# Layer 0's tiles with batch 0's tokens first, its queries made beside the others, more side steps per quartet

## The chip, the core and the metric

The kernel runs on one core of one Trainium2 chip. The metric is the device time of one execution in microseconds, given as the median of three runs. The core has a matrix engine (TensorE, PE), three elementwise engines (VectorE or DVE, ScalarE or ACT, GpSimd or POOL) and SyncE (SP), which issues most DMAs. Each engine works through its own queue in order and waits on semaphores for the others.

## The reference

Four batches of 512 tokens of width 256 go through two layers. Each layer is a cross attention to a context and then a mixture of eight experts, each with its own residual:

```python
x = x + L0_xattn(layernorm(x), ctx)   # one head, MLP 256-1024-256
x = x + L0_ffn(layernorm(x))          # top 2 of 8 experts, 256-1024-256, relu, then W_out
x = x + L1_xattn(layernorm(x), ctx)   # 16 heads of 16, softmax over 512 keys
x = x + L1_ffn(layernorm(x))          # top 1 of 8 experts, 256-512-256, gelu, no W_out
```

What matters here is the passage from the second line to the third. For every token `L0_ffn` sums two experts' outputs, weighted by the gates, and multiplies by `W_out`; this is added to x; x is normalized and multiplied by `Wq` to give the queries. Keys and values come from the context and don't depend on x. Everything is float32.

## The kernel before, in words

**Layer 0's experts.** While layer 0's attention and MLP run, every token's row is sent, once per expert chosen, into a region of `sent` in device memory that belongs to that expert. An expert's rows lie there in the order in which they were sent, so batch 0's are the first of each region. A tile is 256 rows of one expert. One tile, of the expert with the most rows so far, is worked while the last batch is still in its MLP (`pick`, `leave`). `plan` then counts for each expert the tiles still needed (`more`, `count`), sums them up (`end`), and writes for tile number i the expert and the first row: all tiles of expert 0, then all of expert 1, and so on. `leave` prepares what `plan` needs of the tile already taken (`used`, `stride`, `full`, `first`). `full[:, 0, 0:1] = -1.0` makes sure that tile 0 is one of expert 0.

`tiles` works 19 tiles (`usual`), and in an `If` four more, should `plan` have counted more. `run` does per tile: hidden layer (`hide`, 16 matmuls of 256 columns, L587; each float32 matmul is two instructions), loads and turn of the next tile, output (`project`, L600), scaling by the gate (L554) and a scatter of the rows from POOL's queue into `came` (L476), where each row's place follows from its token, batch and pick. Then comes one step of the iterator `also`, which clears the first set of attention buffers (`places`) and fetches batch 0's keys and values (`fetch`).

**Layer 1's attention.** `bring` fetches a batch's two sets of output rows from `came`; it can begin when the scatters have landed. `combine` adds the two, turns them (L1043, L1044) and multiplies by `W_out` (L1068, L1069). `prepare` normalizes (L239 to L252), turns, and makes the queries `qc` (L1086, L1089). `place` lays queries and keys of a batch out for the heads by 16 DMAs each (L1103, L999).

There are 16 groups, four of four heads for each batch. For each group the scores are made twice: by query (`sc`), for each query's maximum over the keys (L1133, kept in `nm`), and, two groups later, by key (`scT`) for the exponentials (L1130). `put_greatest` writes the maxima into qT in between, and `weigh` multiplies the exponentials by the values (`av`, L1146). A group is eight quartets of score matmuls, n = 0 to 7; groups -2 and -1 have maxima only. Between quartets stand the side steps, a list of generators worked in order: a `yield k` asks for k quartets to go by before the next step. Before the change there is a place for a step after n = 1, 5 and 7; after every quartet in groups -2 and -1; after even n too in the last batch; and after n = 2 when more than two generators are in the list. `finish` and `choose` (the attention's output and layer 1's gates) of each batch are side work as well.

Ahead of group -2 the kernel does in this order: all `bring`, `combine` of batch 0, `combine` of batch 1, `prepare` and `place` of batch 0, the clearing of the second set of buffers, part of `combine` of batch 2.

**Who sets the order.** Inside the `manual_schedule` block of the attention PE's order is that of the program. Everything else, in the tiles on all engines and in the attention on the others, is put in order by a planner that walks through the program with its own durations and takes, for a free engine, the earliest instruction of the program that it holds to be ready. `keep_in_program_order` binds an instruction to its place. Buffers of pools that follow each other share addresses; a new one waits for all who used the old. Six banks of PSUM hold scores (`ps_pool`), two hold everything else in the attention (`psT`); `av` keeps one of the two for most of a group.

Of the kernel before, what the change touches and what calls it, by code (L numbers as in the profile page):

```python
# [43 lines left out]
def xattn_ffn_kernel(ctx: ExitStack, tc: tile.TileContext, a: dict, out: bass.AP):  # L44
# [116 lines left out]

    falling = const.tile([P, NT, NE], F32, tag="falling", name="falling")
# [3 lines left out]
    def constants():  # L166
# [14 lines left out]

        nc.gpsimd.memset(full[:, 0, 0:1], -1.0)
# [100 lines left out]
    class Dispatch:  # L283


        def __init__(self, layer, pool, n, func, b1_all):
            self.layer, self.pool, self.group = layer, pool, f"send{layer}"
            self.n, self.func, self.b1_all = n, func, b1_all
            self.w1_all, self.w2_all, self.b2_all = (a[f"L{layer}_ffn_{x}"] for x in ("W1", "W2", "b2"))
            self.kept = []  # L290
            self.seen = pool.tile([P, NT + 1, NE], F32, tag="seen0", name="seen0")
            nc.vector.memset(self.seen[:, 0, :], 0.0)
# [82 lines left out]
        def leave(self):  # L375
# [14 lines left out]
            row = pool.tile([P, 1], I32, tag="row_0", name="row_0")  # L390
            nc.vector.tensor_copy(row, start[:, 0:1])
            self.row_0 = row
            self.stride = pool.tile([P, NE], F32, tag="stride", name="stride")
            nc.vector.tensor_tensor(self.stride, start[:, 1 : NE + 1], start[:, 0:NE], ALU.subtract)
            self.full = pool.tile([P, NE, CAP // TT], F32, tag="full_i", name="full_i")
            nc.vector.tensor_tensor(self.full, over(used, CAP // TT), full, ALU.add)
            self.first = pool.tile([P, TILES0], F32, tag="first_i", name="first_i")
            nc.vector.tensor_scalar(self.first, number[:, :, 0], float(TT), start[:, 0:1], ALU.mult, ALU.add)

        def plan(self):  # L400
# [5 lines left out]
            more = small.tile([P, NE, CAP // TT], F32, tag="more", name="more")  # L406
# [5 lines left out]
            past = small.tile([P, TILES0, NE], F32, tag="past", name="past")  # L412
# [12 lines left out]
            nc.vector.tensor_scalar(e, e, float(NE - 1), None, ALU.min)  # L425
# [90 lines left out]
        def tiles(self, n_tiles, usual, tp, midp, pm_pool, po_pool, also):  # L516
# [46 lines left out]
            def run(first, last):  # L563
# [3 lines left out]
                for i in range(first, last):  # L567
# [7 lines left out]
                    next(also, None)  # L575
# [55 lines left out]
    with tc.tile_pool(name="l0a", bufs=2) as lp, tc.tile_pool(name="l0tmp", bufs=2) as tp, tc.tile_pool(  # L631
# [279 lines left out]
        for b in range(B):  # L911
# [9 lines left out]
            if b < B - 1:  # L921
                together(
                    mlps[b], *(part(g, SCORES) for g in near(attends, 2)), *near(gates, -1), *near(filling, 0)
                )
                if b == B - 2:
# [48 lines left out]
    kTs, vas, qTs = [], [], []  # L974

# [33 lines left out]


    with tc.tile_pool(name="f0tmp", bufs=2) as tp, tc.tile_pool(
# [5 lines left out]
        send.tiles(  # L1017
            TILES0, 2 * N // TT + 3, tp, midp, pm_pool, po_pool, early,
        )
# [7 lines left out]
    with tc.tile_pool(name="l1a", bufs=2) as lp, tc.tile_pool(name="l1s", bufs=1) as sp, tc.tile_pool(  # L1027
# [4 lines left out]
        HALF = S // 2  # L1032
        ctxs, qcs = {}, {}
        send = Dispatch(1, fp, H1, AF.Gelu, a["b1_1_col"])

        def flipped(dst, src, name):

            for c in range(NC):
                if c:
                    yield 0  # L1040
                ps = psT.tile([P, S], F32, tag="psT", name=name)
                for t in range(NT):
                    nc.tensor.transpose(ps[:, ts(t, P)], src[:, t, ts(c, P)], ident)  # L1043
                nc.scalar.copy(dst[:, c, :], ps)  # L1044

        back = came[0].rearrange("(k b p t) d -> k b p t d", k=2, b=B, t=NT)
        ys = {}

        def bring(b):

            y = ys[b] = wpool.tile([P, 2, NT, D], F32, tag="w1" if b % 2 else "w2", name=f"y{b}")
            for k in range(2):
                nc.sync.dma_start(y[:, k, :, :], back[k, b])

        def combine(b):

            xb, y = xs[b], ys[b]
            (nc.gpsimd if b else nc.vector).tensor_tensor(y[:, 0, :, :], y[:, 0, :, :], y[:, 1, :, :], ALU.add)  # L1060
            aT = xtp.tile([P, NC, S], F32, tag="xnT", name="aT")
            yield 2
            yield from flipped(aT, y[:, 0, :, :], "psTr4")
            for t in range(NT):
                yield 0
                po = psT.tile([P, D], F32, tag="psT", name="po4")
                for c in range(NC):
                    nc.tensor.matmul(po, aT[:, c, ts(t, P)], w_out[:, c, :], start=c == 0, stop=c == NC - 1)  # L1068
                nc.vector.tensor_tensor(xb[:, t, :], po, xb[:, t, :], ALU.add)  # L1069

        def prepare(b):

            xb = xs[b]
            xn = sp.tile([P, NT, D], F32, tag="xn", name="xn1")
            xnT = xtp.tile([P, NC, S], F32, tag="xnT", name="xnT1")
            qc = qcs[b] = sp.tile([P, NC, S], F32, tag="qc", name="qc", bufs=2)
            normalize(xn, xb, (nc.vector, nc.scalar, nc.gpsimd, nc.gpsimd)[b])
            nc.gpsimd.tensor_tensor(xb, xb, per_token(bo), ALU.add)
            yield 3
            yield from flipped(xnT, xn, "psTr1")  # L1080
            for m in range(NC):
                for at in range(0, S, HALF):
                    yield 0
                    ps = psT.tile([P, HALF], F32, tag="psT", name="pq")
                    for c in range(NC):
                        nc.tensor.matmul(  # L1086
                            ps, wq[:, c, ts(m, P)], xnT[:, c, at : at + HALF], start=c == 0, stop=c == NC - 1
                        )
                    nc.scalar.activation(qc[:, m, at : at + HALF], ps, AF.Identity, bias=bq[:, m : m + 1])  # L1089

        def place(b):

            qT = qTs[b % 2]
            for _ in fetch(b) if b else early:
                pass
# [316 lines left out]
```

## Time and profile before

| what | us |
|---|---|
| median of three runs (1034.33 to 1038.02) | 1034.34 |
| the profiled execution | 1030.9 |
| its span, first to last instruction | 1029.1 |
| tiles of layer 0, from the first `pm` to the last `po` | 311.2 to 584.7 |
| from there to the first `scT` (group 0) | 584.7 to 649.7 |
| groups 0 to 15, to the last copy of `av` | 649.7 to 920.9 |
| busy: PE, DVE, ACT, POOL | 956.2, 531.9, 358.4, 289.4 |

A row of a profile group gives line, engine, operation, what it writes and reads, the shape and the count, then the busy time in us, the mean ns of one, and the idle time of the engine in front of it with what ended it. In a view in order of time each line starts with the start in us, then the duration in us, and in brackets the idle time of the engine just before. In a table by stretches, the columns are busy us of each engine with its count, PE's granted clock (1.00 is full), the DMA engines' share and GB/s. The chain is the work that ended last, followed back from the last instruction.

### The profile page before, as it was taken

Reading aid. Unit: us, or ns where it says so; the run is one execution under the profiler, and the core shown is the slowest. Engines: PE = TensorE matmul, PEld = TensorE weight load, DVE = VectorE, ACT = ScalarE, POOL = GpSimd, SP = SyncE. Lnnn points to the kernel's source line nnn. Section 1 sums busy time; section 2 is a strip of 40 time slices with the busy share of each in tenths; the row PEclk is TensorE's granted clock in tenths of the full one; section 3 lists DMA queues with packets and bytes.
Section 4 is the critical chain, followed back from the end, with each engine's and each line's share of the span. In section 5 each row is a group of like instructions: output and inputs, shape, how many; then the busy total and the mean of one; then the engine's idle time right before and its main releaser. Section 6 shows DMA issues by size and latency. Waiting matters only on the chain.

```text
span 1029.1 us, 14194 instructions
## 1 busy us (share of the span) xinstructions
PE 956.2 (93%) x4883; PEld 642.2 (62%) x4883; DVE 531.9 (52%) x1384; ACT 358.4 (35%) x646; POOL 289.4 (28%) x330
## 2 busy tenths in 40 slices
PE   5879989999998999999999759999999999998996
PEld 3556757675787888888888645433333333447785
DVE  6675585556652222222222167766777777625232
ACT  4435242223122111221112113466655555572331
POOL 3330153234332212211111176021114121033453
PEclk9889999999999999999999979999999999999998
DMA  6779999963344566556665132000111002034682
GB/s 206 224 185 240 251 253 245 251 151 120 117 142 132 190 210 207 177 182 219 210 206 177 54 159 70 13 11 8 45 33 47 25 22 98 26 98 138 208 247 78
DMA packets 113713, 146.05 MB, mean 142 GB/s; under 512 B 15060, under 2 KB 95197, under 8 KB 113632
## 3 DMA queue, kind: packets, MB, share of 16 engines
q1 hardware_dynamic: 106880, 129.24, 44.2%
q0 software_dynamic: 6336, 14.75, 4.4%
q8 instruction: 43, 0.70, 0.3%
q10 hardware_dynamic: 416, 1.05, 0.3%
q14 instruction: 38, 0.31, 0.1%
HBM read 86.71 MB, written 58.80 MB: 141 GB/s over the span
## 4 chain that ended last, share of the span: by engine, by line
PE 67%; DVE 9%; issue 8%; DMA 7%; POOL 7%; SPq 1%; ACT 1%; POOLq 0%; DVEq 0%; ACTq 0%
PE po L600 13%; PE pm L587 12%; PE sc L1126 12%; PE av L1146 5%; PE po L722 5%; PE pm L716 4%; DMA sent<-rows,slot 2%; PE pm_sid L674 2%; DVE nm L1133 2%; PE pf L682 2%; DMA rows<-sent 1%; PE pd L697 1%; PE pt L812 1%; PE pq L1086 1%; PE po L1180 1%
## 5 line engine op out<-in xcount | busy, mean ns | idle before, releaser
L1133 DVE TENSOR_REDUCE nm<-sc 128x1 f32<-128x512 f32 x256 | 164.9, 683 | 59.8 <-PE scT L1126 57.4
L1130 ACT ACTIVATE ex<-scT 128x512 f32<-128x512 f32 x256 | 138.7, 597 | 107.7 <-PE scT L1126 107.3
L587 PE MATMUL pm<-inT,w 128*128 128x256 f32 x736 | 164.0, 380 | 0.8 <-ACT mid L591 0.5
L600 PE MATMUL po<-w,mid 128*128 128x256 f32 x736 | 163.6, 379 | 0.8 <-ACT mid L591 0.8
L1126 PE MATMUL sc<-kT,qT 32*128 32x512 f32 x512 | 152.9, 642 | 3.8 <-DVE nm L1133 3.6
L587 PEld LDWEIGHTS pm<-inT,w 128*128 128x128 f32 x736 | 139.3, 190 | 21.0 <-ACT mid L591 1.6
L1126 PE MATMUL scT<-qT,kT 32*128 32x512 f32 x512 | 149.8, 642 | 0.0
L600 PEld LDWEIGHTS po<-w,mid 128*128 128x128 f32 x736 | 138.0, 190 | 19.0 <-ACT mid L591 1.2
L476 POOL DMA_INDIRECT came<-y,rows x38 | 37.3, 981 | 218.6 <-DVE y L554 218.6
L554 DVE SCALAR_TENSOR_TENSOR y<-po,rows,y 128x256 f32<-128x256 f32 x54 | 26.1, 483 | 133.5 <-PE po L600 125.4
L1126 PEld LDWEIGHTS sc<-kT,qT 32*128 32x128 f32 x512 | 46.5, 183 | 69.5 <-DVE nm L1133 44.3
L242 POOL TENSOR_TENSOR rstd<-var,halved 128x4 f32<-128x4 f32 (+1 forms) x32 | 28.1, 881 | 213.5 <-DVE var L241 207.5
L591 ACT ACTIVATE mid<-pm,b 128x256 f32<-128x256 f32 x108 | 49.9, 471 | 107.4 <-PE pm L587 92.1
L589 DVE TENSOR_SCALAR mid<-pm,b 128x256 f32<-128x256 f32 x76 | 36.8, 484 | 93.0 <-PE pm L587 93.0
L551 ACT ACTIVATE y<-b,rows 128x256 f32<-128x256 f32 x54 | 24.6, 500 | 168.0 <-DMA b<-in_L_ffn_b 121.7
L335 POOL DMA_INDIRECT sent<-rows,slot x48 | 47.5, 990 | 106.0 <-DVE slot L332 32.3
L1146 PE MATMUL av<-ex,va 128*32 128x512 f32 x512 | 69.5, 612 | 0.0
L716 PE MATMUL pm<-hT,w 128*128 128x512 f32 x128 | 62.3, 611 | 0.5 <-DVE hT L629 0.5
L722 PE MATMUL po<-w,mid 128*128 128x256 f32 x256 | 59.2, 381 | 0.0
L722 PEld LDWEIGHTS po<-w,mid 128*128 128x128 f32 x256 | 47.9, 190 | 9.1 <-issue 3.1
L1126 PEld LDWEIGHTS scT<-qT,kT 32*128 32x128 f32 x512 | 45.1, 183 | 4.1 <-issue 3.5
L1146 PEld LDWEIGHTS av<-ex,va 128*32 128x32 f32 x512 | 10.2, 108 | 48.9 <-issue 37.8
(285 smaller groups left out, 1266.1 us busy)
## 6 DMA issues: line engine op xcount, KB each, us to landing
w<-in_L_ffn_W SPq DMA_DIRECT2D x40, 1024.0 KB, 5.4
sent<-nowhere SPq DMA_DIRECT2D x32, 1161.0 KB, 18.8
w<-in_L_ffn_W SPq DMA_DIRECT2D x22, 512.0 KB, 4.3
rows<-sent SPq DMA_DIRECT2D x27, 258.0 KB, 2.9
y<-came SPq DMA_DIRECT2D x8, 512.0 KB, 9.2
b<-in_L_ffn_b SPq DMA_DIRECT2D x28, 128.0 KB, 7.0
x<-in_x SPq DMA_DIRECT2D x4, 512.0 KB
c<-in_ctx SPq DMA_DIRECT2D x4, 512.0 KB
```

The source lines that it names most:

```text
L335: i = nc.gpsimd.indirect_dma_start(out=sent[self.layer][:, :], out_offset=bass.IndirectOffsetOnAxis(ap=slot[:, t - tts[0], k : k + 1], axi ...
L476: i = nc.gpsimd.indirect_dma_start(out=came[self.layer][:, :], out_offset=bass.IndirectOffsetOnAxis(ap=rows[:, u, TO:ROW].bitcast(I32), ax ...
L587: nc.tensor.matmul(pm, w1[:, c, ts(k, P)], inT[:, c, :], start=c == 0, stop=c == NC - 1)
L589: nc.vector.tensor_scalar(mid[:, k, :], pm, bias[:, k : k + 1], 0.0, ALU.add, ALU.max)
L591: nc.scalar.activation(mid[:, k, :], pm, func, bias=bias[:, k : k + 1])
L600: nc.tensor.matmul(po, mid[:, k, ts(t, P)], w2[:, k, :], start=k == 0, stop=k == n - 1)
L716: nc.tensor.matmul(pm, w1_mlp[:, c, ts(k, P)], hT[:, c, :], start=c == 0, stop=c == NC - 1)
L722: nc.tensor.matmul(po, mid[:, k, ts(t, P)], w2_mlp[:, k, :], start=k == 0, stop=k == HD // P - 1)
L1126: nc.tensor.matmul(sc, stay, move, start=True, stop=True)
L1130: nc.scalar.activation(ex, sc, AF.Exp, scale=1.0 / DH**0.5)
L1133: nc.vector.tensor_reduce(nm[:, t, head, 0:1], sc, AX.X, ALU.max, negate=True)
L1146: nc.tensor.matmul(av[32 * head : 32 * head + 32, :], vas[b % 2][:, t, 4 * g + head, :], exs.pop((t, head)), start=t == 0, stop=t == NT - 1,)
```

## The change

1. `leave` splits layer 0's tiles in two parts. `send.zero` keeps how many rows of batch 0 each expert has. `front` is the number of tiles, behind the one already taken, that hold rows of batch 0, and at least one for expert 0 (`least`). The list of tiles now has all front tiles of all experts first, and then the rest in the old order. `plan` adds what lies in front (`in_front`, `e_front`, `first`).
2. The tiles take a function `also(i)` in place of an iterator. Eleven tiles are the most that the front can have (`FRONT`). After tiles 10 and 11, `bring` fetches batch 0's rows, from POOL's queue; from tile 13 on three steps per tile do `combine`, `prepare` of batch 0; after the last tile `place(0)` follows. The fetched rows, the normalized ones and the queries of batch 0 lie in the tiles' own pool. `flipped`, `combine`, `prepare`, `place` and `bring` move ahead of the tiles unchanged but for the pools and the queue.
3. The attention begins with group -2 right after the other `bring`s and the clearing. All of `combine` and `prepare` of batches 1 to 3 is side work, with `place(1)` as a step of the list. There is a place after n = 2 whenever the list isn't empty, and after n = 6 in groups 0 to 4, in the last batch, and when the list has more than two; groups -2 and -1 take two steps per quartet.
4. The buffers of maxima move from the pool `l1s` to `heads`. In `combine` of batch 1 one exponential of one element is taken after the turn.

```diff
-        nc.gpsimd.memset(full[:, 0, 0:1], -1.0)
+        nc.gpsimd.memset(least, 0.0)
+        nc.gpsimd.memset(least[:, 0:1], 1.0)
...
+            front = least
+            past_used = small.tile([P, NE, CAP // TT], F32, tag="past_used", name="past_used", bufs=1)
+            nc.vector.tensor_tensor(past_used, over(used, CAP // TT), full, ALU.add)
+            if self.zero is not None:
+                more = small.tile([P, NE, CAP // TT], F32, tag="more", name="more", bufs=1)
+                front = small.tile([P, NE], F32, tag="front", name="front")
+                nc.vector.tensor_tensor(more, over(self.zero, CAP // TT), past_used, ALU.is_gt)
+                nc.vector.tensor_reduce(front, more, AX.X, ALU.add)
+                nc.vector.tensor_tensor(front, front, least, ALU.max)
...
+            nc.vector.tensor_scalar(end, end, self.in_front, None, ALU.add)
...
-                    next(also, None)
+                    also(i)
...
+                if b == 1:
+                    n, _ = send.counted("n0")
+                    send.zero = fp0.tile([P, NE], F32, tag="zero", name="zero")
+                    nc.vector.tensor_copy(send.zero, n[:, 0, :])
...
+    for i in range(2):
+        nms.append(heads.tile([P, NT, 4, 32], F32, tag=f"nm{i}", name="nm"))
+        nc.gpsimd.memset(nms[i], 0.0)
...
+    FRONT = (2 * S + NE * (TT - 1)) // TT
...
+        def batch0():
+            yield
+            yield from combine(0)
+            yield from prepare(0, tp)
+
+        zero = batch0()
+
+        def also(i):
+
+            next(early, None)
+            if FRONT <= i + 1 < FRONT + 2:
+                bring(0, i + 1 - FRONT, tp, nc.gpsimd)
+            elif i + 1 < usual:
+                together(part(zero, 3 if i > FRONT + 1 else 0))
+            elif i + 1 == usual:
+                together(zero)
+                together(early)
+                place(0)
+
+        send.tiles(TILES0, usual, tp, midp, pm_pool, po_pool, also)
...
-            for b in range(B):
-                bring(b)
-            prepares, combines = ([g(b) for b in range(B)] for g in (prepare, combine))
-            together(combines[0])
-            next(prepares[0])
-            together(combines[1])
-            together(prepares[0])
-            place(0)
+            for b in range(1, B):
+                for k in range(2):
+                    bring(b, k, wpool, nc.sync)
             together(places(sp))
-            next(prepares[1])
-            together(part(combines[2], 3))
-            side += [combines[2], prepares[1], combines[3]]
-            begun.update(side[:2])
+            combines = [None] + [combine(b) for b in range(1, B)]
+            prepares = [None] + [prepare(b, sp) for b in range(1, B)]
...
+            side += [waiting(8), combines[1], prepares[1], placed(1), combines[2], prepares[2], combines[3], prepares[3]]
+            to_place = [2, 3]
...
+                dense = i < NG + 1 or i // NG == B - 1
...
-                    if n == 0 and i >= 0 and i % NG == 0 and i // NG + 1 < B:
-                        place(i // NG + 1)
-                        if i == 0:
-                            side += prepares[2:]
+                    if to_place and i >= (to_place[0] - 1) * NG and prepares[to_place[0]] not in side:
+                        assert i == (to_place[0] - 1) * NG and n <= 3
+                        place(to_place.pop(0))
...
-                    elif n in (1, 5, 7) or i < 0 or (n % 2 == 0 and i // NG == B - 1) or (n == 2 and len(side) > 2):
+                    elif n in (1, 5, 7) or i < 0 or (n % 2 == 0 and i // NG == B - 1) or (n == 2 and side) or (n == 6 and (dense or len(side) > 2)):
                         step()
+                        if i < 0:
+                            step()
```

## The prediction

> **What bounds the kernel now.** I read the page first, then the busy time by stretch around the seam where layer 0's tiles end, then the instructions in order of time in that seam, then the beat of the attention groups. The page: TensorE (PE) is busy nearly everywhere, and the one deep hole after the start is slices 22 and 23.
>
> ```profile
> PE 956.2 (93%) x4883; PEld 642.2 (62%) x4883; DVE 531.9 (52%) x1384; ACT 358.4 (35%) x646; POOL 289.4 (28%) x330
> PE   5879989999998999999999759999999999998996
> PEclk9889999999999999999999979999999999999998
> ```
>
> The stretches (columns: PE, weight loads, DVE, ACT, POOL busy with counts; granted clock; DMA share; GB/s) show what the hole is:
>
> ```profile
> 560.00:584.70 24.70, 24.67 (x117) 21.38 (x115) 5.48 (x11) 3.75 (x8) 2.92 (x3) 1.00 0.36 119
> 584.70:596.30 11.60, 0.00 (x0) 0.00 (x0) 1.77 (x3) 0.00 (x0) 1.11 (x2) 0.70 0.51 177
> 604.00:612.00 8.00, 1.92 (x9) 1.10 (x7) 6.84 (x7) 0.30 (x1) 6.70 (x6) 0.86 0.00 0
> 622.20:636.00 13.80, 13.13 (x61) 6.83 (x60) 12.17 (x27) 4.19 (x8) 5.18 (x4) 1.00 0.25 58
> 688.40:857.40 169.00, 167.87 (x1174) 62.61 (x1174) 125.88 (x255) 100.12 (x189) 33.30 (x32) 1.00 0.10 28
> ```
>
> In the tiles PE has no free time. Then it stands 11.6 us, works a little, stands 6 us, and from 622 to 650 (the two groups whose scores only feed maxima) DVE is nearly full, while PE's "busy" is the modelled length of four-row-group matmuls and not dense. In order of time:
>
> ```profile
> 577.60 7.07 PE L600 MATMUL po<-w,mid 128*128 128x256 f32 x32
> 589.85 3.96 SPq L1055 DMA_DIRECT2D y<-came  x8
> 594.99 1.23 DVE L1060 TENSOR_TENSOR y<-y 128x1024 f32<-128x1024 f32 x1 [4.20 <-DMA y<-came]
> 596.36 1.94 PE L1043 MATMUL psTr<-ident,y 128*128 128x128 f32 x8 [11.69 <-DVE y L1060]
> 606.33 5.24 DVE L252 TENSOR_SCALAR xn<-x,mv,rstd 128x256 f32<-128x256 f32 x4 [1.16 <-POOL rstd L242]
> 622.25 2.80 PE L1126 MATMUL sc<-kT,qT 32*128 32x512 f32 x8
> 649.69 0.69 PE L1126 MATMUL scT<-qT,kT 32*128 32x512 f32 x1
> ```
>
> The last tile ends at 584.67, its rows land at 589.85, come back at 594.9, are combined, normalized, projected to queries and laid out by 622.25; the first group with weights starts at 649.68. **The seam is 65.0 us.** From there PE's own queue is the chain; the copies of av out of PSUM are its beat:
>
> ```profile
> 671.48 0.58 ACT L1295 COPY avs<-av 128x512 f32<-128x512 f32 x1 [0.15 <-PE av L1146]
> 688.42 0.58 ACT L1295 COPY avs<-av 128x512 f32<-128x512 f32 x1
> 754.82 0.58 ACT L1295 COPY avs<-av 128x512 f32<-128x512 f32 x1
> 771.52 0.58 ACT L1295 COPY avs<-av 128x512 f32<-128x512 f32 x1 [0.39 <-PE av L1146]
> 857.40 0.58 ACT L1295 COPY avs<-av 128x512 f32<-128x512 f32 x1 [0.39 <-PE av L1146]
> ```
>
> Group 1 takes 16.94 us with three query steps in places 1, 5, 7; group 6 takes 16.70 with only two (755 to 772): **an empty odd place still costs some 0.8 us**, for PE then waits for banks of scores to be drained. In the chain a query or output step is 0.86 us after other small work and 1.06 elsewhere, a four-transpose step 0.59 (0.83 in an odd place, where the next quartet waits 0.24). What is left of a group is 14.0 us.
>
> **1. Batch 0 moves among the tiles.** Its PE work there: two turns of 8 transposes at 1.18 us, 16 output matmuls and 16 query matmuls at 0.216 us each (6.9): 9.3 us, with switching 10. The tiles are dense on PE, so all of it is paid. On DVE, ACT and POOL it comes to some 8, 4 and 4 us; the tile stage has DVE at 22%, ACT 15%, POOL 12%, so these hide, unless one stands in front of a tile's own work in its queue. Two such places: the add of y waits for scatter, landing and two fetches; the transposes wait for a normalization. I bound this by 0 (the planner puts them late enough) and 14 us (rival D), and take 1.5, near the case in this trace of ACT holding a tile back (L551 waiting for a bias, PE then idle 0.8 at 321.8). **+11.5.**
>
> The fetches go out on POOL's queue, between scatters: the first waits until tile 10's rows land, and tile 11's scatter waits behind it. [...] The 16 query DMAs (10 us of SP) run under the last tile, all of whose loads are already out: nothing, and without that cover 4 x 0.63 + 2 = 4.5 us.
>
> **2. The seam.** Afterwards score groups -2 and -1 start at once: kT0, qT0 and the maxima buffers are in place. DVE sets the pace, from the tiles' end: first scores and reduce at 2.2; the memset of `seen` has to wait for the last landing (5.5 us of wait at 590.7 before), perhaps 1.5 lost; 28 of the 32 reduces at 0.61 = 17.1; one add of maxima 0.7; four adds of batch 1's output 1.7; its statistics 2.6: 25.8. Then POOL's power 1.05, the small DVE op 0.3, ACT's normalization 2.1, hops 0.5, eight transposes 1.3: 31. One us for small DVE ops held up while POOL runs: 32. POOL clears kT1, qT1, va1 (12.6 us, starting when its scatters have landed, 5.3) in front of or between batch 1's add; in front of it, the add ends at 20.4 instead of 13, the transposes in place (-1, 2) stand, and the seam is 34 to 36. Bounds 28 and 38. **32 - 65 = -33.** [...]
>
> **3. The work the seam no longer hides.** I walked both loops through their places. Before, at group 0's start only one step of batch 3's combine and batches 2 and 3's preparations are left. After, four query steps of batch 1 and all of batch 2 and 3: 15 more steps, one in group 0, 14 in groups 1 to 11 (32 becomes 46). In groups 1 to 11 places 2 and 6 hold 16 steps instead of 1, at 0.59 to 0.86, +11.4; places 1, 5, 7 hold more transposes, -1.3. **+10.1.** With steps closer, less lies between the last output step and the transposes of what is normalized from it. At 764.37 that chain ran from PE's po over POOL (power, then `rows` 4.84) to the transposes at 773.6, some 7.7 us that count. PE has 7.0 us of work in four places, 5.8 in three across a group's start, 4.8 in three inside one. After, batch 3's preparation (4,7 to 5,2), batch 0's choice (7,7 to 8,2) and batch 1's (10,2 to 10,5) have only three: 1.9, 1.9 and 2.9; the qT rows cleared on POOL for batch 3 (1.8 each) may add 0.9 to the second; batch 2 0.5, and the rank matmul two places after the gates 0.8. That is 8.9 against 0.8 before, less 2.5 because DVE and ACT drain banks meanwhile: **+5.6** (0 to 9). Group 0: before 21.8 us, 5 over its sum, DVE being behind with batch 3's adds; after 1.9 more work and some 3 less lag: **-1** (-3 to +3).
>
> **4. The rest.** `leave` has 17 more DVE ops, some 3.6 us, in layer 0 while PE runs 60 po matmuls (13.06 us in the chain at 258.42) and DVE has idle pieces of 1.7 and 2.35 us; in layer 1 in group 14, which has no reduces. `plan` gets one op of 0.17 behind which the tile list waits, but the first rows wait longer for the sends. Same 19 tiles, other order, each still loading its weights. **0** (uncovered: 4). The score buffers' other address costs nothing: two memsets of 0.99 in the tiles; it keeps them clear of memory that the larger tile pool now holds to its end.
>
> **Sum.** 11.5 - 33 + 10.1 + 5.6 - 1 = -6.8. The profiled execution took 1030.9 us around its span of 1029.1 and would take 1024.1; the median is 3.4 above it, and I carry the difference to it: 1034.3 - 6.8 = **1027.5 us**.
>
> **Rivals.** A, the sum: 1027.5, chance 0.46. B, the waits of part 3 and the slack of part 2 don't appear (seam 29, stalls 0, tiles +10): another -10, 1018; for it, the steps' sums agree with the beats to 0.2 us where no normalization intervenes; 0.22. C, the seam's gain is handed on: seam 35, stalls 8: 1033; for it, DVE's 12.17 of 13.80; 0.16. D, the other side: in the tiles every queue is in order, and the planner places batch 0's add and transposes by its own durations. If they stand a fetch and a normalization too early, relus or weights wait behind them: 4.3 + 9.2 less 2.6 of free pm banks, and 7.7 less the same, 16 in place of 1.5: 1042. It decides from 7 us of PE idle in the tiles; against it, no tile from 371 on loses anything; 0.11. E, it doesn't do what it says: the split gives one tile more than 19, and the branch runs it for 14.3 us and the loads: 1043; the counts are cut at the same multiples of 256, so 0.05.
>
> **How the numbers follow.** Timed runs spread up to 0.3%, so 0.5%, 5.2 us, is about what can be told from no change. A with 6 us to either side puts 0.29 under 1029.1 and 0.16 within 0.5%, 0.01 above; B 0.22 faster; C 0.03 faster, 0.11 same, 0.02 slower; D and E 0.01 same, 0.15 slower: faster 0.54, same 0.28, slower 0.18. The range takes in B and C and the lower part of D: 1016 to 1039; A's own is 1021 to 1034.
>
> **What would show it.** Right: no hole of several us at the tiles' end; `y<-came` x2 from POOL among the tiles; the tile stage 10 to 13 us longer; sc matmuls within 3 us of the last po; from there to the first scT about 32; groups 1 to 11 taking 17 to 20 us, about 202 instead of 185.9. Wrong: PE waits inside the tiles (D), a POOL wait in front of batch 1's transposes, groups over 19 us, or a seam over 38.

## The result, and the profile after

The changed kernel takes 1040.78 us (median of 4 runs, 1039.5 to 1041.77) where the kernel before takes 1034.34: ratio 1.0053, 95% interval 1.0028 to 1.0078. It is slower by half a per cent; 1027.5 was predicted, with 1039 as the upper end. Its profiled execution took 1041.0 us around a span of 1039.3, 10.2 more than before. Before's profiled execution lay 3.4 below its median and this one lies on it, so 6.4 of the 10.2 are in the medians.

The page of the changed kernel, its busy time and two rows of its slices:

```profile
PE 969.8 (93%) x4885; PEld 649.7 (63%) x4885; DVE 529.9 (51%) x1419; ACT 359.0 (35%) x647; POOL 291.5 (28%) x333
...
PE   5979989999999999999999988999998999998896
...
PEclk9989999999999999999999968999999999999999
```

The hole of slices 22 and 23 is gone from PE's row, and PE is busy 13.6 us longer: matmuls last longer at a lower clock (below, a score matmul 1.22 us at 0.50 and 0.69 at 1.00). That clock has its dip (6) in slice 24, where groups -2 and -1 now are. By stretches, from one profiled execution of each kernel (the first `pm` of tile 0, the last `po` of the tiles, the first `scT` and the copies of `av` divide them):

| us | before | after | difference | predicted |
|---|---|---|---|---|
| up to the first tile's `pm` | 311.3 | 313.7 | +2.3 | 0 |
| tiles of layer 0 | 273.4 | 282.0 | +8.7 | +11.5 |
| seam | 65.0 | 35.1 | -29.9 | -33 |
| group 0 | 21.8 | 24.1 | +2.3 | -1 |
| groups 1 to 11 | 185.9 | 210.4 | +24.5 | +15.7 |
| groups 12 to 15 | 63.5 | 63.0 | -0.5 | 0 |
| behind the last `av` | 108.2 | 111.0 | +2.8 | 0 |

**The seam**, in order of time (all engines; start, duration, and in brackets the idle time in front):

```profile
597.31 2.57 PE L1200 MATMUL sc<-kT,qT 32*128 32x512 f32 x12 [1.61 <-DVEq L617]
...
601.71 0.34 DVE L422 TENSOR_REDUCE e_front<-past 128x23 f32<-128x184 f32 x1 [5.43 <-DMA came<-y,rows]
601.71 0.07 DVE L295 MEMSET seen<- 128x8 f32 x1
...
602.19 12.04 DVE L1207 TENSOR_REDUCE nm<-sc 128x1 f32<-128x512 f32 x20
...
602.93 9.84 PE L1200 MATMUL sc<-kT,qT 32*128 32x512 f32 x28 [3.05 <-DVE nm L1207]
```

The first scores are there 1.6 us behind the last `po`, as predicted, but the first maximum comes at 602.19, 6.5 us behind it: DVE stands 5.43 us in front of writes into layer 1's small tiles, until the last rows of layer 0 have landed.

**The groups.** The copies of `av` around groups 5, 8 and 10:

```profile
727.37 0.59 ACT L1371 COPY avs<-av 128x512 f32<-128x512 f32 x1
748.34 0.59 ACT L1371 COPY avs<-av 128x512 f32<-128x512 f32 x1
...
783.87 0.59 ACT L1371 COPY avs<-av 128x512 f32<-128x512 f32 x1
806.90 0.59 ACT L1371 COPY avs<-av 128x512 f32<-128x512 f32 x1
825.10 0.59 ACT L1371 COPY avs<-av 128x512 f32<-128x512 f32 x1
846.89 0.59 ACT L1371 COPY avs<-av 128x512 f32<-128x512 f32 x1 [0.16 <-PE av L1220]
```

These three take 21.0, 23.0 and 21.8 us; the other eight of groups 1 to 11 take 17.5 to 18.6. They are the three in which the prediction saw only three places between an output step and the transposes of what is normalized from it. PE and POOL's normalization in group 8, in order of time:

```profile
786.70 1.07 PE L1220 MATMUL av<-ex,va 128*32 128x512 f32 x8
787.32 4.83 POOL L254 TENSOR_SCALAR rows<-x,mv,rstd 128x256 f32<-128x256 f32 x4
788.60 0.33 PE L1066 MATMUL psTr<-ident,rows 128*128 128x128 f32 x1 [0.83 <-POOL rows L254]
789.80 0.33 PE L1066 MATMUL psTr<-ident,rows 128*128 128x128 f32 x1 [0.88 <-POOL rows L254]
791.00 0.33 PE L1066 MATMUL psTr<-ident,rows 128*128 128x128 f32 x1 [0.87 <-POOL rows L254]
792.20 0.48 PE L1066 MATMUL psTr<-ident,rows 128*128 128x128 f32 x1 [0.88 <-POOL rows L254]
792.61 1.22 PE L1200 MATMUL sc<-kT,qT 32*128 32x512 f32 x1
...
795.63 0.69 PE L1200 MATMUL sc<-kT,qT 32*128 32x512 f32 x1
```

The four transposes go at the pace of POOL, which normalizes one quarter of the rows per 1.21 us. Together they wait 3.5 us. Then the score matmuls take 1.22 us instead of 0.69. The stretches of group 5 say why (columns as before: busy time of PE, weight loads, DVE, ACT, POOL, then the granted clock):

```profile
729.00:732.00 3.00, 2.63 (x18) 0.79 (x18) 2.47 (x5) 1.66 (x4) 3.00 (x3) 1.00 0.00 0
732.00:734.00 2.00, 0.91 (x6) 0.59 (x10) 0.00 (x0) 0.21 (x1) 1.92 (x3) 1.00 0.00 0
734.00:737.00 3.00, 3.00 (x16) 1.23 (x12) 1.53 (x4) 1.46 (x3) 1.79 (x1) 0.51 0.03 5
737.00:739.00 2.00, 2.00 (x19) 0.17 (x11) 1.25 (x3) 0.87 (x2) 0.00 (x0) 0.88 0.00 0
```

PE waits some 1.5 us in 729 to 734, and from 734 its clock is 0.51 for three us, while it is busy all the time. (The trace's own clock record has 0.50 from 734.1 to 737.5.)

### The profile page after: what moved, and what is told of

The parts are those of the page before. It is cut to its first block, busy times and chain, and to the rows that moved or that the text cites. A ratio compares the mean times of both kernels' runs of the same rounds, so it can differ in the third digit from the quotient of the medians.

```text
span 1039.3 us, 14216 instructions
## 1 busy us (share of the span) xinstructions
PE 969.8 (93%) x4885; PEld 649.7 (63%) x4885; DVE 529.9 (51%) x1419; ACT 359.0 (35%) x647; POOL 291.5 (28%) x333
## 4 chain that ended last, share of the span: by engine, by line
PE 63%; issue 12%; DMA 8%; DVE 8%; POOL 6%; SPq 1%; ACT 1%; POOLq 0%; DVEq 0%; ACTq 0%
PE po L638 11%; PE pm L625 11%; PE sc L1200 10%; PE po L760 5%; PE pm L754 4%; PE av L1220 4%; PE pm_sid L712 2%; DMA came<-y,rows 2%; PE pf L720 2%; DMA sent<-rows,slot 2%; DVE nm L1207 1%; PE pd L735 1%; DMA rows<-sent 1%; PE psTr L1066 1%; PE pt L850 1%
## 5 line engine op out<-in xcount | busy, mean ns | idle before, releaser
L625 PE MATMUL pm<-inT,w 128*128 128x256 f32 x736 | 167.4, 383 | 3.0 <-ACT mid L629 2.3
L1200 PE MATMUL sc<-kT,qT 32*128 32x512 f32 x512 | 160.5, 696 | 7.1 <-DVE nm L1207 5.3
L1200 PE MATMUL scT<-qT,kT 32*128 32x512 f32 x512 | 153.7, 662 | 0.0
L1200 PEld LDWEIGHTS sc<-kT,qT 32*128 32x128 f32 x512 | 52.1, 197 | 62.6 <-DVE nm L1207 37.7
L589 ACT ACTIVATE y<-b,rows 128x256 f32<-128x256 f32 x54 | 24.5, 500 | 161.0 <-DMA b<-in_L_ffn_b 122.7
L1220 PEld LDWEIGHTS av<-ex,va 128*32 128x32 f32 x512 | 10.3, 109 | 49.7 <-issue 40.0
## 6 DMA issues: line engine op xcount, KB each, us to landing
sent<-nowhere SPq DMA_DIRECT2D x32, 1161.0 KB, 19.6
```

The lines of the kernel that those rows point to most:

```text
L625: nc.tensor.matmul(pm, w1[:, c, ts(k, P)], inT[:, c, :], start=c == 0, stop=c == NC - 1)
L1200: nc.tensor.matmul(sc, stay, move, start=True, stop=True)
L1220: nc.tensor.matmul(av[32 * head : 32 * head + 32, :], vas[b % 2][:, t, 4 * g + head, :], exs.pop((t, head)), start=t == 0, stop=t == NT - 1,)
```

## Experiments

The theory: (T) what the change loses it loses at short waits, in three places. In the groups a normalization comes too late for its transposes, and each such wait also halves PE's clock for some us behind it. At the seam DVE waits for memory. In front of the first tile PE does. Rivals: (R2) only the waits count and not the clock; (R4) the groups are long because they hold more steps; the seam is set by POOL or by the fetch of batch 1 anyway. Ratios are to the kernel before on the same chip; 0.01 is 10.3 us. The changed kernel is at 1.0053, and at 1.0061 where it ran again.

**More distance.** Group by group this undoes the closeness and leaves the steps in.

```diff
 # prepare
-        yield 3
+        yield 4 if b == 3 else 3
 # choose
-            yield 3
+            yield 4 if b < 2 else 3
```

> The preparation of batch 3 and the choices of batches 0 and 1 wait one more quartet, so that their transposes come 6, 4 and 4 quartets behind the last output step instead of 3. Theory T (TensorE waits there for the normalization, 1.5, 3.5 and 2.2 us, and each wait is followed by 3 to 4 us at half clock, about 2 us lost each): the three groups of 21.0, 23.0 and 21.8 us come down to 17.5 to 18.5, no row below 0.9 in the clock there, the whole 10 to 13 us shorter than the changed kernel, 1028 to 1031. Rival R2 (only the waits count, the clock's drop lies under other waits): 6 to 7 us shorter. Rival R4 (the groups are long because they hold more steps): within 2 us of the changed kernel.

Measured: 0.9918 (0.9889 to 0.9948), 14 to 15 us shorter than the changed kernel. The copies of `av`:

```profile
728.06 0.59 ACT L1371 COPY avs<-av 128x512 f32<-128x512 f32 x1
744.72 0.59 ACT L1371 COPY avs<-av 128x512 f32<-128x512 f32 x1
...
780.06 0.59 ACT L1371 COPY avs<-av 128x512 f32<-128x512 f32 x1
797.96 0.59 ACT L1371 COPY avs<-av 128x512 f32<-128x512 f32 x1
815.78 0.59 ACT L1371 COPY avs<-av 128x512 f32<-128x512 f32 x1
834.61 0.59 ACT L1371 COPY avs<-av 128x512 f32<-128x512 f32 x1 [0.39 <-PE av L1220]
```

Groups 5, 8 and 10 take 16.7, 17.9 and 18.8; by stretches of 2 us the clock is 1.00 all through them, though 0.7 us of wait is left in group 8. R4 falls: all steps are still there, and groups 1 to 13 together take 238.6 us instead of 253.0 (229.0 before).

**The clock apart.** TensorE is given work while it waits.

```diff
-    def flipped(dst, src, name):
+    def flipped(dst, src, name, idle=0):
...
+            for k in range(0 if c else idle):
+                nc.tensor.transpose(ps[:, ts(k % NT, P)], ident, ident)
...
-        yield from flipped(xnT, xn, "psTr1")
+        yield from flipped(xnT, xn, "psTr1", 10 if b == 3 else 0)
-            yield from flipped(xnT, to, "psTr3")
+            yield from flipped(xnT, to, "psTr3", (22, 14, 0, 0)[b])
```

> The changed kernel's places are kept; in front of the three late transposes TensorE gets 10, 22 and 14 transposes of the identity, 0.15 us each at full clock, into the bank that the real ones then overwrite, so that it waits for the normalization while at work (1.5, 3.2 and 2.1 us). It adds work and leaves nothing out. T: the waits stay, the clock stays at 1.00 behind them, 4 to 6 us shorter than the changed kernel. R2: the clock's drop costs nothing, within 1 us. Third possibility, that the drop is not from the idle time: the clock still falls to 0.5 there and the time is the same or longer by up to 2 us.

Measured: 1.0041 (1.0021 to 1.0062), that is 1 to 2 us shorter than the changed kernel, with intervals that overlap. The medians alone don't decide between T and R2. The profile shows the place. Group 5 of this kernel:

```profile
728.60:731.60 3.00, 2.40 (x22) 1.67 (x21) 0.10 (x1) 0.59 (x1) 2.92 (x3) 1.00 0.02 5
731.60:734.60 3.00, 3.00 (x27) 1.12 (x20) 2.50 (x6) 1.92 (x4) 1.44 (x1) 1.00 0.00 0
```

The clock stays at 1.00 where it was 0.51, likewise in groups 8 and 10, and the three groups take 19.6, 21.8 and 20.2 us: 4.2 less than in the changed kernel's first profile, at the low end of what was expected, and 6.7 less than in its second (below). One such group alone could be chance: of four profiles with the same waits and without the transposes (two of the changed kernel, the next two experiments) three have half clock in group 5. But all four have it in groups 8 and 10. So the halved clock follows from the idle time, if not each time, and what is left over the first experiment is waiting. The added transposes cost nothing in group 5: where the clock stayed at 1.00 without them, in the next experiment's profile, the group takes the same 19.6 us.

That profile was of the fastest of 16 executions, so its whole span is no measure. The mean granted clock of all timed executions is one: its median is 0.9695 here, 0.9645 and 0.963 in the changed kernel's two series, 0.971 in the first experiment. By an estimate from these, half speed was granted for 10 to 14 us less than in the changed kernel, which is worth 5 to 7 us. Why the medians show only 1 to 2 of them stays open.

**The seam's memory.**

```diff
-        send = Dispatch(1, fp, H1, AF.Gelu, a["b1_1_col"])
+        send = Dispatch(1, heads, H1, AF.Gelu, a["b1_1_col"])
```

> Layer 1's running counts (among them the two small tiles that VectorE writes first behind the layer-0 tiles) are put in memory that no layer-0 tile uses, so VectorE needn't wait for the last rows to land. R3 (that wait of 5.4 us sets the seam's start, and its idle time is why the clock is 0.50 from 602 to 618): first maximum 2 to 3 us behind the last tile instead of 6.5, seam of 35.1 becomes 29 to 31, the clock there near 1.00, whole 4 to 6 us shorter. Rival (the seam is set by POOL's clearing of batch 1's buffers or by the last rows of batch 1 being fetched back, which are not earlier): within 1 us.

Measured: 1.0013 (0.9995 to 1.0030), 4 to 5 us shorter than the changed kernel.

```profile
596.16 1.22 PE L1200 MATMUL sc<-kT,qT 32*128 32x512 f32 x4 [1.59 <-DVEq L617]
597.29 1.29 DVE L1207 TENSOR_REDUCE nm<-sc 128x1 f32<-128x512 f32 x2 [2.13 <-PE sc L1200]
597.97 10.44 PE L1200 MATMUL sc<-kT,qT 32*128 32x512 f32 x36 [0.58 <-issue]
```

The first maximum comes 2.7 us behind the last tile, the seam takes 31.9 instead of 35.1, group 0 22.3. But the expectation of the clock was wrong: it is 0.62 from 602 to 606 and 0.50 to 610 all the same. DVE is busy throughout in those 8 us (4.00 of 4.00 twice), so its reduces cover most of what half clock does there. They don't cover all: six of the profiles here have this edit, and the seam takes 30.5 to 30.9 us in the three where the turn of the maxima (`pt`, four transposes) takes 0.66 us, and 31.9 to 32.5 in the three where it takes 1.11 (in two of them the clock was read there: 0.50).

**Memory among the tiles.**

```diff
+    ... tc.tile_pool(name="f0zero", bufs=1) as zp:
-            yield from prepare(0, tp)
+            yield from prepare(0, zp)
-                bring(0, i + 1 - FRONT, tp, nc.gpsimd)
+                bring(0, i + 1 - FRONT, zp, nc.gpsimd)
```

> Batch 0's three tiles among the layer-0 tiles get a pool of their own, opened last, so that the tile pool has its former size. If the 2.3 us lost ahead of the first tile come from the larger tile pool lying over memory of the picked tile, whose rows must land first: first hidden layer of tile 0 near 311.3 instead of 313.6, whole 2 us shorter. Rival (the other tile order, longer leave and plan, or the score buffers put ahead of the pool do it): no change.

Measured: 1.0038 (1.0018 to 1.0058): 1.6 to 2.4 us, inside the intervals; the trace decides. The first rows turned, in the changed kernel and then here:

```profile
312.19 1.17 PE L510 MATMUL psIn<-ident,rows 128*128 128x128 f32 x8 [2.31 <-DMA came<-mid_s,rows_s]
313.65 2.82 PE L625 MATMUL pm<-inT,w 128*128 128x256 f32 x7 [0.30 <-DVE inT L511]
```

```profile
309.43 0.63 PE L510 MATMUL psIn<-ident,rows 128*128 128x128 f32 x4 [0.68 <-PE po L638]
...
311.55 2.76 PE L625 MATMUL pm<-inT,w 128*128 128x256 f32 x12
```

The wait for the scatter of the tile that was picked early (`mid_s`) is gone, and the first tile starts 2.1 us sooner. But 1.1 of these are there already when the picked tile ends (309.9 and 308.8). From that end to the first `pm` it is 3.8 us, then 2.8; in all profiles with the larger tile pool 3.6 to 5.2 (six, median 4.1), in all with batch 0's tiles in a pool of their own 2.4 to 2.9 (six, median 2.8), in the kernel before 2.1. So the larger pool costs some 1.3 us.

**One part alone.** The kernel before with the split of `leave` and `plan`.

```diff
+            front = least
...
+                nc.vector.tensor_tensor(more, over(self.zero, CAP // TT), past_used, ALU.is_gt)
...
+            nc.vector.tensor_scalar(end, end, self.in_front, None, ALU.add)
...
+                    send.zero = fp0.tile([P, NE], F32, tag="zero", name="zero")
```

> The kernel before with one part of the change alone: leave and plan with the split at batch 0's tokens, and the counts of batch 0 for it; batch 0 itself, the seam and the places of the side steps stay as before. My forecast for this part: 0, so the same as before within 1 us. Rival (the longer leave and plan delay the tile lists): the stretch before the first tile 1 to 2 us longer, or the stretch behind the last attention group 2 to 3 us longer (108.2 before, 109.4 to 113.3 in the changed kernel and its variants), the whole 2 to 4 us longer.

Measured: 1.0014 (0.9990 to 1.0037), no difference that can be measured; 2 us either way stay possible. The rival's two stretches stay open too: the chip of this profile is slow ahead of the first tile (321.3), and the kernel before was not profiled on it, so neither this start nor the 112.0 us behind the last `av` can be held against before's.

**The three edits together**, twice, on two chips that are both slower than the others (1045 for the kernel before). The time is lost ahead of the first tile, which starts at 318 to 322 us there instead of 311 to 315; the tiles take 281 to 283 us in every variant that has batch 0 among them, as elsewhere.

```diff
 # prepare, choose: yield 4 as in the first experiment
+        send = Dispatch(1, heads, H1, AF.Gelu, a["b1_1_col"])
+            yield from prepare(0, zp)
+                bring(0, i + 1 - FRONT, zp, nc.gpsimd)
```

> The three edits of the runs before in one kernel: longer waits ahead of the three late transposes, running counts in memory of their own, batch 0's tiles in a pool of their own. If the losses are three separate places, their gains add: 1040.8 - 14.3 - 5.2 - 2.1 = 1019, ahead of the kernel before by 14 to 15 us (ratio 0.986). Rival (the seam's gain only shows because a later wait absorbs it, or the gains lie under each other): 1023 to 1027, no better than the longer waits alone.

Measured: 0.9914 (0.9881 to 0.9947).

> The combined kernel of the three edits once more. Its first run gave 0.9914 where the sum of the single gains says 0.985 to 0.986; its profile there had group 15 at 11.8 us instead of 8.3, because the rows of a picked tile came late, and 9.5 us of half clock around the start of group 0. If that was the chip's or the execution's: ratio 0.984 to 0.988, group 15 at 8.3 to 9. If the gains don't add: 0.990 to 0.993 again and group 15 long again.

Measured: 0.9895 (0.9858 to 0.9932), group 15 at 11.6 again. So the gains do not simply add: 14 to 17 us of the 21.6. Some 3.3 of what is missing is group 15 in both profiles. There the copy of a picked tile's turned rows comes late, and its matmuls (1.2 to 1.4 us) and those behind the last `av` (1.6) wait. None of the three edits alone has this, the version with 26 transposes below has it too (10.9), and with one more quartet in front of batch 2's choice it is gone; why the copy waits was not traced. The rest of the gap is inside the intervals.

**One more quartet** in front of the transposes of batch 2's choice:

```diff
-            yield 4 if b < 2 else 3
+            yield 4
```

> As the combined kernel, and the choice of batch 2 (group 13) waits one more quartet too. There TensorE waits 1.3 us in all these kernels, in some with half clock for 3 to 4 us behind it (group 24.1 us), in others with full clock (22.6). T: group 13 loses the wait, 1 to 1.5 us shorter than the combined kernel. Rival (group 14 gets the steps, and with them the first loads of layer 1's picked tiles come later): the same or up to 2 us longer.

Measured: 0.9864 (0.9833 to 0.9895), 3 to 5 us shorter than the three edits; group 13 takes 21.7 and group 15 8.4, so most of it came from group 15. The wait that the edit was made for is still there: at 885.6 PE has waited 1.31 us for a maximum, which VectorE makes only behind its normalization for batch 2's choice (`rows`, from 883.58). It never was a wait for the transposes that the edit moves. So the gain is no proof of T, and why group 13 is 0.9 us shorter than 22.6 was not traced.

**Work for TensorE at the seam's end**, added to the three edits:

```diff
-        yield from flipped(xnT, xn, "psTr1")
+        yield from flipped(xnT, xn, "psTr1", 26 if b == 1 else 0)
```

> As the combined kernel, and TensorE gets 26 transposes of the identity (3.8 us at full clock) in front of the transposes of batch 1's normalization, where it waits 4.05 us for ScalarE; nothing is left out. T (this wait is why the seam's end and group 0's first 6 us run at half clock): the clock there at 1.00, seam within 0.3 us, group 0 at 20.5 to 21.8 instead of 22.3 to 24.0, whole 1.5 to 2.5 us shorter than the combined kernel. Rival (VectorE's lag sets group 0, the half clock lies under it): the clock rises, the time stays within 0.7 us.

Measured: 0.9871 (0.9836 to 0.9905). Group 0 takes 22.1, the seam 30.9. The clock still fell, later and for 3.4 us (0.50 from 631.3 to 634.7), because the 26 transposes take 3.1 us and not 3.8, and PE waits another 2.5 us behind them, 2.0 in one piece; where it was left alone it was at half for 6.8 us and more. Group 0 takes 22.3 to 22.4 in three of the four profiles that have the same seam without the transposes (23.5 in the fourth), so nothing of the gain that was expected can be read here. With 42 of them, and with all that helped before:

> All edits that helped: longer waits ahead of four transposes, running counts and batch 0's tiles in memory of their own, and 42 transposes of the identity (6.2 us at full clock) in front of the transposes of batch 1's normalization at the seam's end; with 26 a wait of some 2.7 us was left there and the half clock only came later and shorter (4 us instead of 6.5 to 11). T: no half clock from the seam's end on, group 0 at 20.5 to 21.5 us, ratio to the kernel before 0.982 to 0.986, ahead of the changed kernel by 2%. Rival (the transposes end too late and hold up batch 1's preparation): seam 31 to 33, ratio 0.987 to 0.990, no better than without them.

Measured: 0.9824 (0.9784 to 0.9864), 1016.7 us where the kernel before has 1033.4. This version beats both. Over the version with the four longer waits and without the transposes (0.9864) it gains 4 us, with intervals that overlap. Its stretches in the seam and group 0:

```profile
602.00:614.00 12.00, 12.00 (x41) 7.53 (x40) 10.97 (x19) 0.00 (x0) 11.93 (x8) 0.50 0.76 281
...
618.00:627.90 9.90, 9.69 (x74) 7.21 (x66) 7.44 (x20) 2.40 (x5) 4.74 (x5) 1.00 0.15 51
627.90:648.76 20.86, 20.86 (x129) 7.80 (x132) 12.19 (x19) 12.31 (x25) 3.10 (x5) 1.00 0.09 20
```

The last row is group 0: 20.9 us at full clock, against 24.1, 7.6 us of which were at 0.50 (630.8 to 638.4). The seam takes 32.5 here, with half clock from 598.3 to 615.3. The transposes hold the clock at the seam's end; in group 13 it is halved all the same, for 3.4 us from 878.2, behind the same wait of 1.31 us (23.1 us).

**A faster normalization in place of more distance.**

```diff
-        normalize(xn, xb, (nc.vector, nc.scalar, nc.gpsimd, nc.gpsimd)[b])
+        normalize(xn, xb, (nc.vector, nc.scalar, nc.gpsimd, nc.scalar)[b])
-            normalize(to, xs[b], nc.gpsimd if b < B - 2 else nc.vector)
+            normalize(to, xs[b], nc.scalar if b < B - 2 else nc.vector)
```

> The changed kernel with its places; only the last pass of three normalizations (preparation of batch 3, choices of batches 0 and 1) goes from POOL (4.8 us) to ScalarE (2.1 us). T: the normalization is some 2.7 us shorter, so the waits of 1.5, 3.5 and 2.2 us nearly vanish, the clock stays at 1.00 there, groups 5, 8 and 10 come to 18 to 19.5 us, the whole 8 to 12 us shorter than the changed kernel. Rival (ScalarE has exponentials for every quartet, so its 2.1 us hold up scores and the av copies instead): groups 5, 8 and 10 stay over 20 us, the whole within 4 us of the changed kernel.

Measured: 1.0087 (1.0049 to 1.0126), no gain: the rival, though not in the groups that it named. Groups 5, 8 and 10 do get shorter (19.9, 19.8, 20.7), but groups 4 and 7, each in front of one of them, go from 18.6 and 18.0 to 22.4 and 24.0. ScalarE takes its instructions in the order of its queue here: the four wait 1.70 us for the statistics, with the exponentials and the copy of `av` behind them:

```profile
725.17 0.60 ACT L1204 ACTIVATE ex<-scT 128x512 f32<-128x512 f32 x1 [0.99 <-PE scT L1200]
727.47 2.07 ACT L249 ACTIVATE xn<-x,less,rstd 128x256 f32<-128x256 f32 x4 [1.70 <-DVE less L247]
729.45 0.57 ACT L1204 ACTIVATE ex<-scT 128x512 f32<-128x512 f32 x1
729.92 0.57 ACT L1371 COPY avs<-av 128x512 f32<-128x512 f32 x1
```

**The changed kernel again**, nothing edited.

> The changed kernel once more, beside the two below on one chip, and for a second profile. Expected: ratio 1.005 to 1.006 to the kernel before; groups 5, 8 and 10 at 20 to 24 us with half clock for 3 to 4 us behind each wait, seam 35, first tile late by 2 us, as in its first profile. If one of these is not there again, it was that execution's and not the change's.

Measured: 1.0061 (1.0034 to 1.0088). The seam takes 35.0, group 0 23.7, groups 5, 8 and 10 20.9, 24.4 and 23.0, the first tile starts at 315.3: all there again. Groups 8 and 10 are longer than the first time because the clock is halved for 6.8 us behind their waits (793.0 to 799.8 in group 8, where two pairs of exponentials come 3.0 us apart that came 2.0 apart the first time) instead of 3.4.

## Why the prediction was wrong

The first `pm` and the tiles. **Part 1** said +11.5 and it was +8.7: no fetch held a tile back (the two `y<-came` go out at 475.65 and 489.76, as described, and land after 5.5 and 4.3 us), and PE's only wait of the change in this stage is 0.8 us for batch 0's normalized rows, where 1.5 was taken. Rivals D and E did not come: no idle PE in the tiles, no twentieth tile. (D's 9.2 us are the median to landing of the eight `y<-came` of the kernel before, its 4.3 the time from the last scatter to the first of them, 585.54 to 589.85.) **Part 4** named the larger tile pool and priced nothing for it; it cost some 1.3 of the 2.3 in front of the first tile, where its memory was last read by a scatter. The 2.8 behind the last `av` need not be the change's: this stretch is 108.2 before, 108.2 in the best version, which has the same `leave` and `plan`, and 109.3 to 113.3 in the others; what makes it vary was not traced.

**Part 2** had the seam at 32 and it was 35.1. The pace of the chain was right to 1 or 2 us: without DVE's wait it is 31.9 (30.5 to 32.5 in six profiles), where the prediction without its 1.5 has 30.5. The failed term is "perhaps 1.5 lost". DVE stands 5.4 us, of which 3.2 reach the seam's end, and the wait holds not only the memset of `seen` but `e_front` and its like: `leave` of layer 1, put down under group 14, has ops whose inputs are constant since the split, and the planner ran those at the seam. The feared order on POOL did not come (batch 1's add started at 606.25, ahead of the strips). Nor did the 1 us for small DVE ops beside POOL: before, `var` took 1.49 us beside a memset on POOL (603.68) and `less` 2.30 beside an add (620.66); here they take 0.17 and 0.16, with POOL idle (625.90, 627.23).

**Part 3** had two terms. The moved steps were right: +10.1 predicted, and with the waits taken out groups 1 to 13 are 9.6 over the kernel before (11.2 if the 1.6 us are left out that half clock costs in before's group 12). **The step that failed is the second, +5.6 for waits.** It was 14.4 (253.0 less 238.6), and the medians agree (14 to 15). The three places and their causes were named rightly, and so was the idle time: 1.9, 2.8 and 2.9 us forecast, 1.5, 3.5 and 2.2 read. What went wrong is the price, in two ways. Of 8.1 (8.9 less the 0.8 of before) 2.5 was taken off because other engines drain banks meanwhile, where the runs give 8.7 with nothing taken off (247.3 with TensorE kept busy, less 238.6). And nothing was put down for the clock, which is the other 5.7 (253.0 less 247.3; 1.5 of it in group 13, which the edit doesn't touch). The split rests on one profile of each kernel: with the changed kernel's second profile the clock's part is 8.3, and in the medians it is 1 to 2.

The rows that the prediction shows of the attention have the clock at 1.00 (622.20 to 636.00, 688.40 to 857.40), but PE is busy 13.13 of 13.80 and 167.87 of 169.00 us in them, so they say little of what comes behind a wait. The single waits in groups 5, 8, 10 and 13 are 0.5 to 1.3 us. The trace of the kernel before has the case of such a wait, in group 12, just behind the last stretch that the prediction read (PE in order of time, then two stretches):

```profile
863.73 0.69 PE L1126 MATMUL sc<-kT,qT 32*128 32x512 f32 x1 [1.07 <-DVE nm L1133]
```

```profile
862.30:865.70 3.40, 2.33 (x14) 1.03 (x16) 3.33 (x11) 1.19 (x2) 0.14 (x1) 1.00 0.11 39
865.70:869.10 3.40, 3.40 (x20) 0.34 (x12) 2.00 (x5) 1.08 (x2) 0.00 (x0) 0.50 0.06 16
```

One wait of 1.1 us, then half clock for 3.4 us; the group takes 20.5 us, and 18.9 in the run of one part alone, where two pairs of exponentials come 2.1 us apart (877.52 and 879.64) that come 3.1 apart here (867.21 and 870.30). The same came behind waits of groups 5 to 13, and once at group 0, where PE waits 4.0 us for ScalarE. Group 0 was predicted at -1 and came at +2.3; with the clock held it is 20.9, -0.9, which is the forecast. On the 17 us of half clock inside the seam, taking nothing was right to within 2 us.

**The sum.** From -6.8 to +10.2 are 17.0: stalls +8.8 and the moved steps -0.5 in groups 1 to 13 (groups 12 and 13 are in here), group 0 +3.3, seam +3.1, first tile +2.3, tiles -2.8, the stretch behind the last `av` +2.8; the last two groups are even. The medians differ by 6.4, not 10.2: 3.8 of the 17.0 come with the choice of executions, and group 13 (1.5) and the stretch behind the last `av` (2.8) are where such a difference was seen. Rival C had the seam to 0.1 us and too little in the stalls. No rival on the slower side had this mechanism, though the waits stood in the working; the clock had no term in the sum. Of the signs of being wrong that it named, one came: groups over 19 us.

## What to carry over

The work that moved out of the hole was paid almost in full in the dense stretches (8.7 us in the tiles, 9.6 in groups 1 to 13), and what made or broke the trade was the distance between a producer and its consumer once the steps stood closer: one more quartet of distance was worth 14 us, and the faster normalization nothing, because ScalarE's queue waited in another place (groups 4 and 7 went from 18.6 and 18.0 us to 22.4 and 24.0). Price a wait of a dense TensorE as itself plus the slower clock that may follow (here 1.2 to 1.6 us for each 3.4 us at half clock, one or two of them behind a wait), and take a row of the profile as evidence only for a stretch with the same waits in it. Look for what each new tile's memory was used for last: two of the three losses were first uses of a tile that waited for a scatter out of an older one (DVE 5.4 us at the seam, some 1.3 us ahead of the first tile).

## What the runs showed of the hardware

A wait of 1.3 us was followed by half clock in some executions and not in others. Group 13 in the changed kernel, and in the one with TensorE kept busy in the three other groups:

```profile
893.77:895.77 2.00, 0.69 (x10) 0.09 (x2) 2.00 (x6) 0.52 (x2) 0.00 (x0) 1.00 0.00 0
...
897.77:901.77 4.00, 4.00 (x22) 1.43 (x20) 1.62 (x4) 1.79 (x4) 0.00 (x0) 0.57 0.00 0
```

```profile
886.80:888.80 2.00, 0.69 (x10) 0.08 (x2) 2.00 (x6) 0.52 (x2) 0.00 (x0) 1.00 0.00 0
...
890.80:894.80 4.00, 4.00 (x34) 1.62 (x32) 2.26 (x4) 2.68 (x5) 0.00 (x0) 1.00 0.00 0
```

The same wait, PE busy 0.69 of 2 us in both, is followed by a clock of 0.57 for 4 us in one and 1.00 in the other. The wait is for a maximum on VectorE, and is 1.3 us in all fourteen profiled executions, wherever batch 2's choice stands. In eight of them the clock is halved for 3.4 us behind it (group 13 takes 24.1 to 24.2 us, 23.1 in the best version), in six, before's among them, it stays at 1.00 (22.6, 21.7 with the choice moved).

The halved stretches that were read between the seam's end and the last `av` last 3.4 us or a multiple of it: 3.4 in the kernel before (654.1 to 657.5, 865.7 to 869.1) and in groups 5, 8, 10 and 13 of the changed kernel, 10.2 at its seam's end (628.3 to 638.5), 6.8 there with one more quartet and 10.2 with the three edits. So one wait's price came in steps here. Group 8, with the same waits, takes 23.0 us with 3.4 us at half clock and 24.2 to 24.4 with 6.8; with TensorE kept busy and the clock at 1.00 it takes 21.8. And inside the seam the clock is at 0.50 for up to 17 us (601.0 to 618.0 in the changed kernel), also where PE counts as busy throughout (12.00 of 12.00 us in the best version), so busy time as the profile models it does not tell when the clock falls.
